# A 7x7 depthwise filter moved from VectorE to TensorE, with banded matrices streamed from HBM

## The chip, the cores and the metric

The kernel runs on one core of one Trainium2 chip. The metric is the device time of one execution in microseconds (us), the median of all its executions. Ratios are the mean time of one kernel's fast runs over that of the other's in the same rounds, so they are not quite the ratio of the medians that stand beside them.

## The reference

Eight images of 56 x 56 tokens with 192 channels, all in fp32, go through four layers. Each adds its result to its input, and each begins with a group norm. The change concerns layer 3:

```
y = conv_general_dilated(gn(x), dw_kernel, 'SAME', feature_group_count=192) + dw_bias   # 7x7, one filter per channel
y = (y - mean) * rsqrt(var + 1e-6) * ln_gamma + ln_beta                                 # over the channels
y = gelu(y @ w0 + b0) @ w1 + b1                                                         # 192 -> 768 -> 192
x = x + y * gamma                                                                       # gamma = 1e-6
```

One thing to keep in mind: with gamma at 1e-6 the comparison with the reference hardly sees layer 3.

## The kernel before

A program of the core goes image by image, layer by layer. The image lies in SBUF with channels on partitions, as two halves of 96. The filter is 49 multiply-adds per half on VectorE, over a padded copy of the image:

```
for k in range(2):
    pad = ...                        # GpSimd clears the border, ScalarE writes the normed image into it
    yk = y[:, k].rearrange("p (h w) -> p h w", w=W)
    for tap in range(49):
        i, j = divmod(tap, 7)
        win = pad[:, i:i + H, j:j + W]
        wt = vec("dw", 49 * k + tap, HC)
        if tap == 0:
            nc.vector.tensor_scalar(yk, win, wt, vec("dwb", k, HC), ALU.mult, ALU.add)
        else:
            nc.vector.scalar_tensor_tensor(yk, win, wt, yk, ALU.mult, ALU.add)
center_and_scale(y, ...)             # layer norm: TensorE, VectorE, ScalarE
for t in range(NTT): ...             # the MLP on TensorE, GELU on ScalarE, store of x
```

Of the kernel before, what the change touches and what calls it, by code (L numbers as in the profile page):

```python
# [18 lines left out]
NT = H * W          # tokens of one image  # L19
HC = 96             # channels are held as two halves of 96 partitions  # L20
TT = 392            # tokens per matmul: seven rows
NTT = NT // TT
D1 = 576            # expanded width of layer 0
DCH = [(0, 128), (128, 128), (256, 128), (384, 128), (512, 64)]
NSUB = D1 // 64
HEADS, HD, WN = 6, 32, 49
C2 = 384
EXP = 768

# Per-partition vectors, packed by the host as columns of one [128, NV] array.  # L30
# [5 lines left out]
    ("dw", 98), ("dwb", 2), ("g3", 2), ("be3", 2), ("b0", 6), ("b1", 2), ("ls", 2),  # L36
]
VOFF = {}
NV = 0
# [5 lines left out]
def _reversed(ap):  # L45
    """The access pattern that runs backwards over the last dimension."""
    dims = [list(d) for d in ap.ap]
    step, num = dims[-1]
    return bass.AP(ap.tensor, ap.offset + (num - 1) * step, dims[:-1] + [[-step, num]])
# [3 lines left out]
def kernel(ctx: ExitStack, tc: tile.TileContext, a: dict, out: bass.AP):  # L53
# [13 lines left out]
    # ---------------------------------------------------------------- constants  # L67
# [36 lines left out]
    # layer scale times its bias, so that (y + b1) * ls = y * ls + lsb  # L104
# [5 lines left out]
    # Toeplitz matrices of layer 0 and attention bias + mask of layer 1, made once and kept in HBM.  # L110
# [3 lines left out]
    # ---------------------------------------------------------------- helpers  # L114
    def gn_stats(x, pool, psum):
        """Per-channel scale and shift of the group norm over (H, W, 6 channels)."""
        st = pool.tile([HC, 2, NTT, 6], F32, name="gn_st")
        mv = pool.tile([HC, 2, 2], F32, name="gn_mv")
        for k in range(2):
            for t in range(NTT):  # L120
                nc.vector.bn_stats(st[:, k, t, :], x[:, k, bass.ts(t, TT)])
            nc.vector.bn_aggr(mv[:, k, :], st[:, k].rearrange("p t s -> p (t s)"))
        gm = psum.tile([HC, 2], F32, name="gn_ps", tag="gn_ps", bufs=1)
        nc.tensor.matmul(gm, gmat, mv[:, :, 0], start=True, stop=True)
        mean = pool.tile([HC, 2], F32, name="gn_mean")
        nc.vector.tensor_copy(mean, gm)
        d = pool.tile([HC, 2], F32, name="gn_d")
        nc.vector.tensor_tensor(d, mv[:, :, 0], mean, ALU.subtract)
        nc.vector.tensor_tensor(d, d, d, ALU.mult)
        nc.vector.tensor_tensor(d, d, mv[:, :, 1], ALU.add)  # L130
        gv = psum.tile([HC, 2], F32, name="gn_ps2", tag="gn_ps", bufs=1)
        nc.tensor.matmul(gv, gmat, d, start=True, stop=True)
        sc = pool.tile([HC, 2], F32, name="gn_sc")
        nc.scalar.activation(sc, gv, AF.Sqrt, bias=eps5[0:HC])
        nc.vector.reciprocal(sc, sc)
        sh = pool.tile([HC, 2], F32, name="gn_sh")
        nc.vector.scalar_tensor_tensor(sh, mean, -1.0, sc, ALU.mult, ALU.mult)
        return sc, sh

    def center_and_scale(X, P, NC, mean_w, eps, pool, psum):  # L140
        """X <- (X - mean) / sqrt(var + eps) over the channels (partitions x NC), in place."""
        vps = psum.tile([128, 2, 512], F32, name="ln_var", tag="ln_var", bufs=1)
        for t in range(NTT):
            g, j = divmod(t, 2)
            xs = X[:, :, bass.ts(t, TT)]
            mp = psum.tile([P, TT], F32, name="ln_mean", tag="ln_b", bufs=2)
            for k in range(NC):
                nc.tensor.matmul(mp, mean_w, X[:, k, bass.ts(t, TT)], start=(k == 0), stop=(k == NC - 1))  # L148
            nc.vector.tensor_tensor(xs, xs, mp.unsqueeze(1).to_broadcast([P, NC, TT]), ALU.subtract)  # L149
            sq = pool.tile([P, NC, TT], F32, name="ln_sq", bufs=2)  # L150
            nc.scalar.activation(sq, xs, AF.Square)  # L151
            for k in range(NC):
                nc.tensor.matmul(
                    vps[32 * g:32 * g + 32, j, 0:TT], mean_w[:, 0:32], sq[:, k, :],
                    start=(k == 0), stop=(k == NC - 1),
                )
        rs = pool.tile([128, 2, TT], F32, name="ln_rs", bufs=1)
        nc.scalar.activation(rs, vps[:, :, 0:TT], AF.Sqrt, bias=eps)
        nc.vector.reciprocal(rs, rs)
        for t in range(NTT):  # L160
            g, j = divmod(t, 2)
            xs = X[:, :, bass.ts(t, TT)]
            bp = psum.tile([P, TT], F32, name="ln_rstd", tag="ln_b", bufs=2)
            nc.tensor.matmul(
                bp, ones[32 * g:32 * g + 1, 0:P], rs[32 * g:32 * g + 1, j, :], start=True, stop=True
            )
            nc.vector.tensor_tensor(xs, xs, bp.unsqueeze(1).to_broadcast([P, NC, TT]), ALU.mult)

    # ---------------------------------------------------------------- set-up of layer 0
    def build_toeplitz():  # L170
        coef = dram.tile([2, D1, 112], F32, name="coef")
        with tc.tile_pool(name="tz", bufs=2) as pool, tc.tile_pool(name="tz_ps", bufs=2, space=PSUM) as psum:
# [6 lines left out]
            # powers of the decay, 0..55, then laid out by lag: column k is lag 55 - k  # L179
# [17 lines left out]
            for i in range(2):  # L197
# [19 lines left out]
                # Hankel rows by overlapping reads, turned into Toeplitz rows by a backward copy  # L217
# [9 lines left out]
    # ---------------------------------------------------------------- set-up of layer 1  # L227
    def build_bias_mask():
        with tc.tile_pool(name="bm", bufs=2) as pool, tc.tile_pool(name="bm_ps", bufs=1, space=PSUM) as psum:
            rev = pool.tile([WN, WN], F32, name="rev", bufs=1)  # L230
            nc.gpsimd.dma_start(rev, a["rev49"])
            # rows by reversed query: offsets (i', j') + (im, jm) into the reversed table
# [27 lines left out]
    # ---------------------------------------------------------------- layer 0  # L260
    def layer0(x, b):
        with ExitStack() as st:
# [16 lines left out]
            for c, (d0, M) in enumerate(DCH):  # L279
                # q * v by channel, in rows of 64 columns (the last 8 are zero)  # L280
# [9 lines left out]
                # o[w, d, h] = sum_w0 T1[w0, w] qv[w0, h] + sum_h0 qv[h0, w] T2[h0, h], as one  # L290
                # product per channel: rows 0..55 hold the w0, rows 64..119 the h0
# [43 lines left out]
                # gate, and the part of the output projection of these channels  # L335
# [16 lines left out]
    # ---------------------------------------------------------------- layer 1  # L352
    def layer1(x, b):
        with ExitStack() as st:
# [8 lines left out]
            # scores: heads of one 32-row group of the array share a bank, windows of a pair are  # L363
            # 64 partitions apart; the rows between them are zero
# [5 lines left out]
            def rolled(g):  # L370
                """(rows of the group, rows and columns of the image) of a rolled row of windows."""
# [5 lines left out]
            for g in range(8):  # L377
                bm = pool.tile([128, 3, 8 * WN], F32, name="bm")
                nc.sync.dma_start(bm.rearrange("p a b -> p (a b)"), bmask[g])
                # window after window, each of 7 x 7 tokens  # L380
# [61 lines left out]
                # keys onto partitions: et[m, (h % 3, pair, h // 3), query of both windows]  # L442
# [37 lines left out]
    # ---------------------------------------------------------------- layer 2  # L480
    def layer2(x, b):
        with ExitStack() as st:
# [11 lines left out]
            for m in range(3):  # L494
# [25 lines left out]
                # four running averages (their gain is applied to the sum)  # L520
# [32 lines left out]
    # ---------------------------------------------------------------- layer 3  # L553
    def layer3(x, b):
        with ExitStack() as st:
# [3 lines left out]
            y = pool.tile([HC, 2, NT], F32, name="y3", bufs=1)  # L559
            for k in range(2):  # L560
                pad = pool.tile([HC, H + 6, W + 6], F32, name="pad3")
                nc.gpsimd.memset(pad[:, 0:3, :], 0.0)
                nc.gpsimd.memset(pad[:, H + 3:H + 6, :], 0.0)
                nc.gpsimd.memset(pad[:, 3:H + 3, 0:3], 0.0)
                nc.gpsimd.memset(pad[:, 3:H + 3, W + 3:W + 6], 0.0)
                nc.scalar.activation(
                    pad[:, 3:H + 3, 3:W + 3], x[:, k].rearrange("p (h w) -> p h w", w=W), AF.Identity,
                    bias=sh[:, k:k + 1], scale=sc[:, k:k + 1],
                )
                yk = y[:, k].rearrange("p (h w) -> p h w", w=W)  # L570
                for tap in range(49):
                    i, j = divmod(tap, 7)
                    win = pad[:, i:i + H, j:j + W]
                    wt = vec("dw", 49 * k + tap, HC)
                    if tap == 0:
                        nc.vector.tensor_scalar(yk, win, wt, vec("dwb", k, HC), ALU.mult, ALU.add)
                    else:
                        nc.vector.scalar_tensor_tensor(yk, win, wt, yk, ALU.mult, ALU.add)  # L578
# [41 lines left out]
def _lay_out(inp):  # L620
    f = {k: np.asarray(v) for k, v in inp.items()}

    def cols(v, p, n):
        """A vector as n columns of p partitions, in 128 rows."""
# [19 lines left out]
        "dwb": cols(l3("dw_bias"), HC, 2), "g3": cols(l3("ln_gamma"), HC, 2), "be3": cols(l3("ln_beta"), HC, 2),  # L644
        "b0": cols(l3("b0"), 128, 6), "b1": cols(l3("b1"), HC, 2), "ls": cols(l3("gamma"), HC, 2),
    }
    for i in (1, 2):
# [3 lines left out]
    dw = np.zeros((128, 98), np.float32)  # L651
    dw[:HC] = l3("dw_kernel").reshape(49, 2, HC).transpose(2, 1, 0).reshape(HC, 98)
    v["dw"] = dw
# [17 lines left out]
        "w0": halves(l3("w0")), "w1": blocks(l3("w1")),  # L671
# [19 lines left out]
```

## Time and profile before

| | before |
|---|---|
| time, us (2 runs) | 14,654.9 and 14,661.6 |
| PE busy | 8,491.7 us, 58% |
| VectorE busy | 7,833.3 us, 53% |
| bytes read from HBM | 201 MB |
| filter stage, one image | 344.6 us, VectorE alone |

The prediction shows the page's lines and the filter stage. For contrast here are the windows of the first image on both sides of it: the end of layer 2, then the layer norm and the MLP of layer 3. The columns are: window, its length, busy time (and instructions) of PE, PEld, DVE, ACT, POOL, then granted TensorE clock, DMA share, GB/s.

```profile
1529.30:1559.30 30.00, 29.97 (x85) 14.45 (x84) 10.00 (x15) 2.19 (x4) 0.00 (x0) 0.93 0.00 0
...
1903.90:1955.60 51.70, 44.87 (x85) 13.81 (x85) 19.57 (x16) 16.29 (x22) 0.00 (x0) 0.67 0.00 0
1955.60:2083.30 127.70, 126.31 (x377) 67.18 (x376) 9.99 (x17) 41.67 (x69) 0.00 (x0) 0.98 0.06 17
```

TensorE sets the pace on both sides and VectorE in between. The stages do not overlap, so a time won or lost in the filter stage counts in full, eight times.

### The profile page before, as it was taken

How to read it: one execution, taken by the hardware profiler on the slowest of the kernel's cores; microseconds unless marked ns; L12 is line 12 of the kernel's file. 1: busy time of each engine (PE TensorE's matmuls, PEld its weight loads, DVE VectorE, ACT ScalarE, POOL GpSimd, SP SyncE). 2: the span in 40 equal slices, each digit the busy share in tenths (PEclk: the TensorE clock that was granted, in tenths of full speed). 3: DMA queues.
4: the chain of work that ended last, by engine and by line, in shares of the span. 5: the costliest groups of instructions: out<-in, count | busy, mean ns of one | idle time of the engine just before them, and what ended most of it. 6: DMA issues, size and time to landing. Idle time of an engine off the chain costs nothing.

```text
span 14692.5 us, 108024 instructions
## 1 busy us (share of the span) xinstructions
PE 8491.7 (58%) x46978; PEld 4935.2 (34%) x46978; DVE 7833.3 (53%) x6307; ACT 2537.9 (17%) x3928; POOL 170.7 (1%) x331
## 2 busy tenths in 40 slices
PE   2873278731887308873088631886338852388524
PEld 1642046410454105541055310553115431154312
DVE  2237832478324792247922488225872358623685
ACT  0211022210221102211022110221112111122111
POOL 2000000000000000000000000000000000000000
PEclk9776577765877658776577765867667676677756
DMA  7100011000110001100010000100001000010000
GB/s 134 29 12 9 0 26 24 14 7 0 26 24 14 7 0 26 24 14 7 0 35 15 14 7 1 34 18 11 7 3 33 18 11 7 5 40 10 9 0 7
DMA packets 107622, 249.45 MB, mean 17 GB/s; under 512 B 73238, under 2 KB 85812, under 8 KB 95724
## 3 DMA queue, kind: packets, MB, share of 16 engines
q1 hardware_dynamic: 103148, 234.09, 7.0%
q0 software_dynamic: 4000, 8.46, 0.2%
q8 instruction: 368, 6.03, 0.2%
q14 instruction: 106, 0.87, 0.0%
HBM read 201.38 MB, written 41.12 MB: 17 GB/s over the span
## 4 chain that ended last, share of the span: by engine, by line
PE 54%; DVE 38%; issue 3%; ACT 2%; DMA 0%; DVEq 0%; ACTq 0%; POOL 0%; SPq 0%; POOLq 0%
DVE y L578 17%; PE pj L273 10%; PE op L329 7%; PE y L345 5%; DVE mixed L519 5%; PE ph L588 4%; PE po L596 3%; PE tph L316 3%; PE mm L404 3%; PE mmv L416 2%; PE ln_mean L148 2%; PE et_ps L447 2%; PE ot L341 2%; DVE tmp L534 2%; PE po L546 2%
## 5 line engine op out<-in xcount | busy, mean ns | idle before, releaser
L578 DVE SCALAR_TENSOR_TENSOR y<-pad,vecs_sb,y 96x3136 f32<-96x3136 f32 x768 | 2610.0, 3475 | 0.6
L148 PE MATMUL ln_mean<-y,mean 96*96 96x392 f32 x256 | 128.7, 649 | 2648.4 <-DVE y L578 2648.4
L273 PE MATMUL pj<-xn,w_pqv_sb 96*128 96x392 f32 (+1 forms) x3840 | 1508.2, 544 | 35.5 <-DVE xn L268 33.9
L329 PE MATMUL op<-rt,lt 120*56 120x56 f32 x9216 | 1003.3, 303 | 223.3 <-DVE o L332 113.5
L329 PEld LDWEIGHTS op<-rt,lt 120*56 120x56 f32 x9216 | 904.0, 210 | 320.8 <-DVE o L332 141.4
L148 PEld LDWEIGHTS ln_mean<-y,mean 96*96 96x96 f32 x256 | 46.0, 203 | 2725.9 <-DVE y L578 2659.0
L273 PEld LDWEIGHTS pj<-xn,w_pqv_sb 96*128 96x128 f32 (+1 forms) x3840 | 705.5, 193 | 607.1 <-issue 164.9
L345 PE MATMUL y<-pp,w_o_sb 128*96 128x392 f32 (+1 forms) x1280 | 697.6, 682 | 231.0 <-DVE pp L342 231.0
L148 PE MATMUL ln_mean<-mixed,mean 128*128 128x392 f32 x384 | 189.0, 636 | 1071.9 <-DVE mixed L536 1070.6
L519 DVE SCALAR_TENSOR_TENSOR mixed<-pad,vecs_sb,mixed 128x3136 f32<-128x3136 f32 x192 | 670.1, 3490 | 5.7
L447 PE MATMUL et_ps<-ident,e 128*49 128x128 f32 x1536 | 349.1, 407 | 557.0 <-DVE e L441 556.1
L503 PE MATMUL pin<-xn,w_in_sb 96*128 96x392 f32 x768 | 339.2, 610 | 508.5 <-ACT pad L507 475.2
L342 DVE TENSOR_TENSOR pp<-pp,ot 128x392 f32<-128x392 f32 (+1 forms) x320 | 179.5, 561 | 829.1 <-PE ot L341 541.5
L332 DVE COPY o<-op 56x448 f32<-56x448 f32 x288 | 177.6, 617 | 829.2 <-PE op L329 829.2
L602 DVE TENSOR_TENSOR x<-x,z 96x392 f32<-96x392 f32 x128 | 72.0, 563 | 940.8 <-ACT z L600 940.8
L588 PE MATMUL ph<-y,w_sb 96*128 96x392 f32 x1536 | 568.0, 525 | 0.0
L350 DVE TENSOR_TENSOR x<-x,y 96x392 f32<-96x392 f32 x512 | 286.0, 559 | 466.6 <-PE y L345 454.8
L151 ACT ACTIVATE ln_sq<-y 96x784 f32<-96x784 f32 x64 | 54.8, 857 | 2768.8 <-DVE y L149 2739.5
L289 DVE TENSOR_TENSOR qv<-qs,vs 128x392 f32<-128x392 f32 (+1 forms) x320 | 180.2, 563 | 633.1 <-ACT vs L287 633.1
L596 PE MATMUL po<-hid,w_sb 128*96 128x392 f32 x1536 | 516.2, 492 | 0.0
L316 PE MATMUL tph<-ident,qv 64*56 64x64 f32 x4032 | 473.5, 296 | 40.2 <-ACT rt L312 34.7
L148 PEld LDWEIGHTS ln_mean<-mixed,mean 128*128 128x128 f32 x384 | 82.9, 234 | 1171.1 <-DVE mixed L536 1090.0
(157 smaller groups left out, 12471.6 us busy)
## 6 DMA issues: line engine op xcount, KB each, us to landing
lt<-toep SPq DMA_DIRECT2D x72, 896.0 KB, 6.9
rt<-toep SPq DMA_DIRECT2D x72, 784.0 KB
bm<-bmask SPq DMA_DIRECT2D x64, 588.0 KB, 3.7
x<-in_x_dram SPq DMA_DIRECT2D x16, 1176.0 KB, 8.2
out_dram<-x SPq DMA_DIRECT2D x64, 294.0 KB, 2.6
toep<-tzt SPq DMA_DIRECT2D x18, 896.0 KB, 6.2
hk<-coef SPq DMA_DIRECT2D x18, 784.0 KB
bmask<-bmt POOLq DMA_DIRECT2D x8, 588.0 KB, 3.1
```

The source lines that it names most:

```text
L148: nc.tensor.matmul(mp, mean_w, X[:, k, bass.ts(t, TT)], start=(k == 0), stop=(k == NC - 1))
L273: nc.tensor.matmul(ps[0:M], w_pqv[:, k, which, d0:d0 + M], xn[:, k, bass.ts(t, TT)], start=(k == 0), stop=(k == 1),)
L316: nc.tensor.transpose(tp[:, i, :], qv[q0:q0 + 64, :, 8 * grp + i], ident[q0:q0 + 64, q0:q0 + 64])
L329: nc.tensor.matmul(op[:, i, :], lt[0:120, d, :], rt[0:120, d, :], start=True, stop=True)
L345: nc.tensor.matmul(y, w_o[0:M, c, k * HC:(k + 1) * HC], pp[0:M], start=True, stop=True)
L404: nc.tensor.matmul(ps, w_qkv[:, k, c0:c0 + HC], xf[:, k, :], start=(k == 0), stop=(k == 1))
L447: nc.tensor.transpose(tp[:, j, :], e[:, 4 * i + j, :], ident)
L503: nc.tensor.matmul(ps.rearrange("p h w -> p (h w)"), w_in[:, k, m * 128:(m + 1) * 128], xn[:, k, bass.ts(t, TT)], start=(k == 0), stop=(k ...
L519: nc.vector.scalar_tensor_tensor(loc3, win, wt, loc3, ALU.mult, ALU.add)
L578: nc.vector.scalar_tensor_tensor(yk, win, wt, yk, ALU.mult, ALU.add)
L588: nc.tensor.matmul(ps, w0[:, k, m * 128:(m + 1) * 128], y[:, k, bass.ts(t, TT)], start=(k == 0), stop=(k == 1),)
L596: nc.tensor.matmul(ps, w1[:, m, k * HC:(k + 1) * HC], hid[:, m, :], start=(m == 0), stop=(m == 5))
```

## The change

The intent is to take the filter from VectorE to TensorE, which is busy for 3.86 of the 344.6 us of that stage. Two image rows (112 tokens) go onto partitions by transposes. For each channel a banded matrix turns those 112 inputs into two output rows; four matrices (j) cover the seven filter rows. A channel has only 28 pairs of rows, so its matmul fills 32 columns of the array, and four channels go to four column groups. The bands are made on the host and streamed from HBM; all 192 channels' bands are 39 MB. A 113th row of the contraction, all ones in z, carries the bias.

```diff
-            y = pool.tile([HC, 2, NT], F32, name="y3", bufs=1)
-            for k in range(2):  # ... pad, and 49 multiply-adds on VectorE
+            xp = ...   # normed image, one empty row above and below
+            z = pool.tile([128, C * ZS + 8], F32, name="z", bufs=1)       # 112 tokens x (channel, pair of rows)
+            # ... 58 transposes, 12 copies into z, borders cleared, ones in row 112
+            for T in range(C // 16):
+                k, p0 = divmod(16 * T, HC)
+                cv = psum.tile([128, 4, ZR], F32, name="cv", tag="ln_b")
+                for g in range(4):
+                    bd = pool.tile([ZR + 1, 4, 4 * ZR], F32, name="band", bufs=3)   # ZR = 112
+                    nc.sync.dma_start(bd, a["band"][4 * T + g])
+                    for j in range(4):
+                        for u in range(4):
+                            c = 16 * T + 4 * u + g
+                            nc.tensor.matmul(
+                                cv[32 * u:32 * u + 32, g, :], z[0:ZR + 1, c * ZS + j:c * ZS + j + 32],
+                                bd[:, u, j * ZR:(j + 1) * ZR], start=(j == 0), stop=(j == 3),
+                            )
+                yc = ...   # copy of cv, VectorE and ScalarE in turn
+                for u in range(4):
+                    nc.sync.dma_start(yd[...], yc[32 * u:32 * u + 28])    # to HBM, and back by channel:
+                if p0 == HC - 16:
+                    nc.sync.dma_start(y[:, k], yd[...])
```

The rest of the diff takes comments out, drops the filter weights from the resident constants and builds the bands on the host.

## The prediction

> **What bounds the kernel now.** I read the page's busy shares, then the chain of work that ended last, then that chain in order of time for one image, then windows of that image, and last the DMA queues and issues, because the change moves work from VectorE to a stream from HBM.
>
> ```profile
> PE 8491.7 (58%) x46978; PEld 4935.2 (34%) x46978; DVE 7833.3 (53%) x6307; ACT 2537.9 (17%) x3928; POOL 170.7 (1%) x331
> ...
> PE 54%; DVE 38%; issue 3%; ACT 2%; DMA 0%; DVEq 0%; ACTq 0%; POOL 0%; SPq 0%; POOLq 0%
> ...
> L578 DVE SCALAR_TENSOR_TENSOR y<-pad,vecs_sb,y 96x3136 f32<-96x3136 f32 x768 | 2610.0, 3475 | 0.6
> ```
>
> No engine is full over the whole span: the images run one after another, each through four layers, and within a layer one engine sets the pace. The filter of layer 3 is 768 VectorE instructions of 3.475 us, with VectorE idle only 0.6 us before all of them. The chain in time shows one image:
>
> ```profile
> 1529.34 29.94 PE po L546 x84
> 1559.85 4.30 DVE gn_st L121 x9
> ...
> 1581.16 20.43 DVE y L578 x7
> ...
> 1604.85 295.53 DVE y L578 x87
> 1900.40 3.49 DVE y L578
> 1903.94 5.61 PE ln_mean L148 x8
> ```
>
> Layer 2 ends at 1559.3 (1529.34 + 29.94); the layer norm behind the filter starts at 1903.9. Windows on those borders:
>
> ```profile
> 1559.30:1903.90 344.60, 3.86 (x8) 1.75 (x8) 339.55 (x123) 6.26 (x3) 1.63 (x8) 0.51 0.00 0
> ```
>
> The columns are busy PE, PEld, DVE, ACT, POOL, then granted clock, DMA share, GB/s. So the stage is 344.6 us per image, 8 x 344.6 = 2,757 us in all, VectorE alone; TensorE and the DMA engines do nothing in it. That is all that the change can win. A replacement must finish in under 344.6 us per image.
>
> [...] The change brings 384 loads of a band tile of 113 partitions (112 rows and one row for the bias). [...]
>
> [...]
>
> ```profile
> q1 hardware_dynamic: 103148, 234.09, 7.0%
> ...
> lt<-toep SPq DMA_DIRECT2D x72, 896.0 KB, 6.9
> rt<-toep SPq DMA_DIRECT2D x72, 784.0 KB
> ```
>
> Data packets, one per contiguous row: lt 72 x 64, rt 72 x 56, toep 18 x 64, hk 18 x 56 x 64, bm 64 x 128, out 64 x 192, x 16 x 96, coef 8 x 128 + 2 x 64, six constants 416 rows: 97,888. What is left of 103,148 is 5,260 completion packets. The 250 loads and stores whose partition count 16 divides account for 4,000; the other 90 (rt and hk, 56 partitions) for 1,260, which is 14 each. 14 is the largest divisor of 56 up to 16. [...]
>
> [...] The trace's packet records give the duration of one packet where it is not slowed by others: 66 ns for 1,568 bytes, 181 for 4,704, 467 for 12,544, 533 for 14,336. That is a line, 8.5 ns plus 27.3 bytes per ns[...]; within one engine the packets follow each other without a gap (in the stores to out the next starts 3 ns before to 2 ns after the last ends). With 16 engines at once the whole is less than 16 times that:
>
> ```profile
> 1368.00:1370.00 2.00, 0.00 (x0) 0.00 (x0) 1.97 (x2) 0.00 (x0) 0.00 (x0) 0.50 1.04 245
> 2684.00:2686.00 2.00, 0.00 (x0) 0.00 (x0) 2.00 (x5) 0.00 (x0) 0.00 (x0) 0.50 0.93 310
> ```
>
> [...]
>
> **The change part by part, for one image.**
>
> Removed: 96 multiply-adds of 3.475 us (333.6), two first taps of 1.905, two pad activations of 3.05 and their waits. All of the 344.6 us goes, except the group-norm statistics (11 us) that begin the stage in both.
>
> Added on VectorE, ScalarE and TensorE: two scalings (1.9 us each, as the xn rows take), 58 transposes of 96 x 112 and 12 copies of some 0.6 us, 768 matmuls of 112 columns, 12 copies of 128 x 448. The po chain runs 24 matmuls of 392 columns in 7.90 us at a clock of 0.98, 0.84 ns a column; 112 columns are then 0.09 us, or 0.19 at half clock (estimates). The 16 matmuls that one band feeds take 1.5 to 3 us even if the column groups overlapped not at all. All of this is small.
>
> Added on the queue: 48 band loads of 113 rows x 7,168 bytes (810 KB). One row is 8.5 + 7168 / 27.3 = 271 ns on one engine; 113 rows are 30.6 us. With three buffers there are always two loads queued behind the one that runs: the built program issues band n+3 when the 16 matmuls of band n are done, and each block's four stores to yd come behind the bands two ahead. So the one engine does not run dry, and the stream takes 48 x 30.6 = 1,469 us. The engine's share of the yd stores (two of 28 rows, 4 packets of 25 ns each, 48 times: 9.6 us) and of the first y load (6 x 467 ns: 2.8 us) is in the same ring: 12 us.
>
> Head: the first band waits for layer 2's last output matmul, because its buffer lies where layer 2's tiles were. So the stream starts at 1559.3 + 1.0 (x needs 1.0 us from issue to its first packet). Statistics and transposes lie beside it, for the first matmuls can wait until about +35 us while only three bands fill.
>
> Tail: after the last band 3 us of matmuls, 0.6 copy, four store issues at 0.45, 2.2 landing, and the second y load 6.6: about 15 us.
>
> Sum: 1 + 1,469 + 12 + 15 = 1,497 us in place of 344.6: +1,152 us per image. Everything before 1559.3 and after 1903.9 is unchanged, and the images do not overlap here. 14,658 + 8 x 1,152 = 23,876, rounded to 23,880 us.
>
> **The rivals.**
>
> 1. *All 16 engines carry the bands*[...]. For it: the author surely meant it so, and 245 GB/s would bring a band in 3.3 us. Then the stage would be some 34 us until the transposes are done, 45 further bands at 3.3 to 3.7 us, up to 12 block ends at 5 us where stores hold the queue, and the tail: 215 to 275 us instead of 344.6, a gain of 0.55 to 1.0 ms, ending at 13.65 to 14.1 ms. Against it: the 14 completions of a 56-row load.
>
> 2. *One engine, at another speed.* My packet times come from moments with other engines at work, but the fast ones are on a straight line of bytes, so I take them as the engine's own rate. [...] A lone engine [...] say 22 GB/s, gives 36.8 us and 26.3 ms. The 20.8 GB/s (310 / (16 x 0.93)) of the second window above is with 16 engines and some slow packets, so this is the less likely side.
>
> 3. *The queue adds bubbles*: the stores to yd wait for a copy, and bands behind them are not issued meanwhile. If the engine ran dry at each of 12 blocks for 8 us, 8 x 96 us = 0.8 ms more: 24.6 ms. Against it: two bands of 30 us each are queued at that moment.
>
> 4. *TensorE becomes the bound* by matmuls [...]. Even at 300 ns each, without overlap, 768 take 230 us, hidden under the stream [...]; under rival 1 it would cancel most of the gain.
>
> **Range and chances.** The answer is almost binary. I give the one-engine branch 0.92. Inside it the rate moves the time by 0.36 ms for 1 us of a band; 28 to 32.5 us and small bubbles give 22.9 to 24.9 ms, my range, for 8 times in 10. Rival 1 with a good outcome has 0.06, and 0.02 is left for it with its gain eaten by TensorE or the queue.
>
> **What would show it.** Right: in the filter's stage a DMA share near 0.06 (1 of 16) at 26 to 27 GB/s; a band landing every 30 to 31 us, and near 90 us from issue to landing with three queued; q1 with 113 + 1 packets per band load, so 384 single completions; the chain that ended last in layer 3 on DMA, with TensorE waiting for band; VectorE's busy time down by some 2.6 ms. Wrong: 113 + 16 packets per load, a share near 1, a band each 3 to 4 us. A band well off 30.6 us would mean that the engine's rate is mis-sized; a rate right but a stage longer than 48 bands would mean bubbles.

That the band loads of 113 rows run on one engine was an estimate of mine at that point: the trace of before shows 14 completions for each load of 56 rows, 14 being the largest divisor of 56 up to 16, and holds no load of 113 rows.

## The result, and the profile after

The changed kernel took 23,906.03 us (2 runs, 23,905.1 to 23,907.0) against 14,658.25; the ratio is 1.631, 95% interval 1.626 to 1.636.

From the page of the changed kernel: busy time by engine; the DMA queue of the sync engine; the chain that ended last, by engine and by line; and the group of the new matmuls (count, busy us, mean ns, then the idle time before them and what ended it).

```profile
PE 9217.6 (39%) x59730; PEld 5506.4 (23%) x59730; DVE 5283.6 (22%) x5635; ACT 2543.1 (11%) x4008; POOL 208.3 (1%) x315
...
q1 hardware_dynamic: 197100, 583.63, 8.1%
...
PE 35%; DMA 18%; SPq 17%; another core or an unknown queue 13%; DVE 12%; issue 2%; ACT 1%; DVEq 0%; ACTq 0%; POOL 0%; POOLq 0%
DMA band<-in_band_dram 18%; SPq L614 14%; PE pj L274 6%; PE op L330 4%; PE y L346 3%; DVE mixed L520 3%; SPq L600 2%; PE ph L629 2%; PE po L637 2%; PE tph L317 2%; PE mm L405 2%; PE cv L604 2%; PE mmv L417 1%; PE ln_mean L149 1%
...
L604 PE MATMUL cv<-band,z 113*32 113x112 f32 x12288 | 667.0, 393 | 11034.3 <-DMA band<-in_band_dram 11034.3
```

VectorE lost 2,550 us of work, as intended, and TensorE gained 726. But TensorE stood still for 11,034 us before the new matmuls, all of it for bands. (The count 12,288 is twice the 6,144 matmuls of the source: in this trace each of these fp32 matmuls shows as two instructions, while the 464 transposes, 58 an image, show as one each.)

The chain of the first image in order of time (start, length, what) shows the pace:

```profile
1522.44 29.95 PE po L547 x84
1552.52 32.64 DMA band<-in_band_dram
...
1615.85 1.72 PE cv L604 x32
1617.57 28.89 another core or an unknown queue
1646.50 1.72 PE cv L604 x32
1648.22 28.88 another core or an unknown queue
1677.14 1.77 PE cv L604 x32
...
3045.17 6.82 DMA y<-yd
...
3052.03 5.61 PE ln_mean L149 x8
```

The matmuls of one band (32 instructions) take 1.72 us, then TensorE waits until 30.65 us after the last band came, and so on: 1646.50 - 1615.85 = 30.65, 1677.14 - 1646.50 = 30.64. The words "another core or an unknown queue" are the profile's for a landing that it can't assign; the waits in the group above name the band. Blocks of the chain that it books on the sync queue's issues (L614) have the same inside: four bands with a block's stores take 1800.50 - 1677.14 = 123.4 us, 30.8 each. The stage runs from 1552.4 to 3052.0, 1,499.6 us in place of 344.6. One period as a window:

```profile
1646.00:1677.20 31.20, 1.77 (x36) 1.38 (x40) 0.00 (x0) 0.00 (x0) 0.00 (x0) 0.50 0.06 26
```

A DMA share of 0.06 is one engine of 16, and that one moves 26 GB/s. The queue's packets say the same: 197,100 - 103,148 = 93,952 more than before. Stores to yd (384 x (112 + 14)) and loads of y (16 x (96 + 16)) are 50,176 of them; the other 43,776 are 384 x 114, that is 113 rows and one completion per band. In the packet records the completions are packets of 4 bytes, 11,276 in this trace and 5,260 in that of before. A row of 7,168 bytes takes 273 ns in the median and 272 at the least.

### The profile page after: what moved, and what is told of

Read it like the earlier page. It is cut to its first block, busy times and chain, and to the rows that moved or that the text cites. A ratio compares the mean times of both kernels' runs of the same rounds, so it can differ in the third digit from the quotient of the medians.

```text
span 23905.2 us, 134629 instructions
## 1 busy us (share of the span) xinstructions
PE 9217.6 (39%) x59730; PEld 5506.4 (23%) x59730; DVE 5283.6 (22%) x5635; ACT 2543.1 (11%) x4008; POOL 208.3 (1%) x315
## 3 DMA queue, kind: packets, MB, share of 16 engines
q1 hardware_dynamic: 197100, 583.63, 8.1%
## 4 chain that ended last, share of the span: by engine, by line
PE 35%; DMA 18%; SPq 17%; another core or an unknown queue 13%; DVE 12%; issue 2%; ACT 1%; DVEq 0%; ACTq 0%; POOL 0%; POOLq 0%
DMA band<-in_band_dram 18%; SPq L614 14%; PE pj L274 6%; PE op L330 4%; PE y L346 3%; DVE mixed L520 3%; SPq L600 2%; PE ph L629 2%; PE po L637 2%; PE tph L317 2%; PE mm L405 2%; PE cv L604 2%; PE mmv L417 1%; PE ln_mean L149 1%
## 5 line engine op out<-in xcount | busy, mean ns | idle before, releaser
L604 PE MATMUL cv<-band,z 113*32 113x112 f32 x12288 | 667.0, 393 | 11034.3 <-DMA band<-in_band_dram 11034.3
L604 PEld LDWEIGHTS cv<-band,z 113*32 113x32 f32 x12288 | 509.3, 167 | 11195.2 <-DMA band<-in_band_dram 8747.5
L317 PEld LDWEIGHTS tph<-ident,qv 64*56 64x56 f32 x4032 | 397.9, 161 | 85.6 <-ACT rt L313 40.1
L448 PEld LDWEIGHTS et_ps<-ident,e 128*49 128x49 f32 x1536 | 262.2, 188 | 610.2 <-DVE e L442 563.9
L342 PEld LDWEIGHTS ot<-ident,o 56*128 56x128 f32 (+1 forms) x2240 | 282.8, 190 | 465.5 <-issue 350.3
L342 PE MATMUL ot<-ident,o 56*128 56x56 f32 (+1 forms) x2240 | 367.5, 295 | 24.6 <-ACT o L335 24.6
L405 PE MATMUL mm<-xr,w_qkv_sb 96*96 96x392 f32 x1024 | 371.2, 518 | 14.7 <-DVE xn L168 9.2
```

The lines of the kernel that those rows point to most:

```text
L317: nc.tensor.transpose(tp[:, i, :], qv[q0:q0 + 64, :, 8 * grp + i], ident[q0:q0 + 64, q0:q0 + 64])
L342: nc.tensor.transpose(ot[0:M, i, :], o[:, 0:M, 7 * t + i], ident[0:W, 0:W])
L405: nc.tensor.matmul(ps, w_qkv[:, k, c0:c0 + HC], xf[:, k, :], start=(k == 0), stop=(k == 1))
L448: nc.tensor.transpose(tp[:, j, :], e[:, 4 * i + j, :], ident)
L604: nc.tensor.matmul(cv[32 * u:32 * u + 32, g, :], z[0:ZR + 1, c * ZS + j:c * ZS + j + 32], bd[:, u, j * ZR:(j + 1) * ZR], start=(j == 0), s ...
```

## The experiments

The theory: 113 has no divisor from 2 to 16, so a band load runs on one DMA engine, and that alone makes the stage long. The rivals: the 311 MB of bands are too much whatever the engines; TensorE, granted a clock of 0.50 in the stage, comes right behind; the waits of the queue.

**112 rows and the bias row apart.** The same bytes, tile and matmuls, two transfers a band.

```diff
-                    nc.sync.dma_start(bd, a["band"][4 * T + g])
+                    nc.sync.dma_start(bd[0:ZR], a["band"][4 * T + g, 0:ZR])
+                    nc.sync.dma_start(bd[ZR:ZR + 1], a["band"][4 * T + g, ZR:ZR + 1])
```

> The same bytes, the same 113-row tile and the same matmuls, but each band comes by two transfers, 112 rows and then the one bias row. Theory (one engine of 16 because 113 has no divisor up to 16): the 112 rows run on 16 engines, a band lands every 3.3 to 3.8 us instead of 30.6, the filter stage takes 215 to 275 us, the time is 13.6 to 14.1 ms, under the kernel before. Rival a (the 311 MB of the stream, or HBM, are the bound): the time stays at 23.9 ms. Rival b (TensorE [...] is the bound just behind the stream): the stage stays above 345 us and the time above 14.66 ms.

Measured: 13,827.65 us, ratio to the kernel before 0.9435 (0.942 to 0.9451). The stage is 241.4 us. From its page, the sync queue, and a window in the middle of the stage:

```profile
q1 hardware_dynamic: 203244, 583.66, 17.2%
```

```profile
1620.00:1640.00 20.00, 9.04 (x176) 7.10 (x172) 0.62 (x1) 0.00 (x0) 0.00 (x0) 0.50 0.83 221
```

The queue has 203,244 - 197,100 = 6,144 packets more, 16 a band: 112 + 16 and 1 + 1 in place of 113 + 1. So the band's rows now run on 16 engines, and 221 GB/s are moved in place of 26. That rules the bytes out as the cause: the same 311 MB now fit into a stage that is shorter than the one on VectorE.

**118 rows.** The band gets five zero rows; 118 is 2 x 59.

```diff
-                    bd = pool.tile([ZR + 1, 4, 4 * ZR], F32, name="band", bufs=3)
+                    bd = pool.tile([118, 4, 4 * ZR], F32, name="band", bufs=3)       # matmuls read bd[0:ZR + 1]
```

> The band is padded with five zero rows to 118 = 2 x 59 rows, in one transfer; the matmuls read the first 113. 4% more bytes. Theory (largest divisor up to 16): two engines, 59 rows of 271 ns each, 16.0 us a band, 48 of them 768 us, the stage near 795 us in place of 1,500, the time 18.1 to 18.5 ms, and 118 + 2 packets a band. Rival a (bytes): 4% longer than the changed kernel's stage, 24.4 ms. Rival c (any other count than 113 is spread over all 16 engines): 14 ms as with 112 + 1 rows.

Measured: 18,321.17 us (one run). Chain, first image:

```profile
1528.91 29.94 PE po L547 x84
...
2348.81 7.16 DMA y<-yd
...
2356.01 5.61 PE ln_mean L149 x8
```

The stage is 2356.0 - 1558.9 = 797 us, forecast 795. The queue has 199,404 packets, 6 a band more than with 113 rows: 118 + 2 in place of 113 + 1. More bytes, two engines, half the time: with 113, 118 and 112 rows the count of completions is the largest divisor up to 16 (1, 2 and 16), and the stage takes 1,499.6, 797 and 241.4 us.

**One band for all.** No stream; the result is wrong.

```diff
+            bd = pool.tile([ZR + 1, 4, 4 * ZR], F32, name="band", bufs=1)    # loaded once per image, used by all matmuls
             for T in range(C // 16):
                 for g in range(4):
-                    bd = pool.tile(...); nc.sync.dma_start(bd, a["band"][4 * T + g])
```

> Wrong result on purpose: one band is loaded per image and all 768 matmuls of the filter use it, so the stream is gone and all else stays (transposes, matmuls, copies, stores, reload). It measures the stage without its stream. Theory: statistics and transposes 34 us, 48 times 1.72 us of matmuls as the changed kernel's trace shows them = 83 us, tail 15 us, together 120 to 140 us, the time 12.9 to 13.1 ms. If the stores' waits or the copies set the pace of a block, the stage is above 180 us and the time above 13.3 ms.

Measured: 12,615 us (one run), less than forecast. The stage without its stream is 1648.6 - 1559.8 = 88.9 us. The miss is the clock: I had taken 1.72 us a band from the changed kernel, whose granted clock is 0.50 in the window above, but in the run without the stream TensorE is granted 1.00 (the first window of the next experiment), and a band takes 0.82 us. So TensorE was not near being the bound of the changed kernel.

**The same, group after group.** What do the four column groups bring? Only the order of the matmuls changes.

```diff
-                    for j in range(4):
-                        for u in range(4):
+                    for u in range(4):
+                        for j in range(4):
```

> As the run with one band (wrong result on purpose, no stream), but the 16 matmuls of a band are issued group after group, so that four in a row go to the same column group. With the groups in turn, 128 instructions [...] took 3.27 us at full clock, 25.5 ns each. If column groups run beside each other, [...] the 1,536 instructions of an image 30 to 33 us more, the time 12.85 to 12.9 ms. If the 25.5 ns are only an issue pace and nothing overlaps, 12.6 ms as before. Rival: the order hardly matters, because the fourth is followed by another group.

Measured: 12,853.57 us (one run). A window of the matmuls in the run with groups in turn, then in this one:

```profile
1595.00:1615.00 20.00, 16.45 (x642) 15.16 (x640) 1.88 (x3) 1.06 (x2) 0.00 (x0) 1.00 0.25 55
```

```profile
1600.00:1620.00 20.00, 20.00 (x392) 20.00 (x389) 0.63 (x1) 1.06 (x2) 0.00 (x0) 1.00 0.16 34
```

Both at full clock. In turn: 16.45 us for 642 instructions, 25.6 ns each. Group after group: 20 us for 392, 51 ns each. So the order is worth a factor of 2.0, and the stage grows from 88.9 to 118.2 us. The time is the forecast one, but by luck: the forecast assumed a pace, which no trace had shown, for an instruction that follows another on its group. The start times in the two traces say 96 ns.

In turn, starts come in fours: three steps of 6 to 8 ns, then a longer one, and from a start to the fourth after it is 96 ns in the median. In the po chain, 24 fp32 instructions of 392 columns in 7.90 us, one starts every 329 ns, which is 94 ns for 112 columns (an estimate from this chain). So four instructions run beside each other, each at its own pace of 96 ns, and the four column groups bring 96 / 25.6 = 3.7. Group after group, the eight instructions of a group start within 413 ns in place of 8 x 96 = 766, so even there about two neighbouring groups overlap. (The trace does not name the groups; that the four are four groups is read from the order in the source.)

The 25.6 ns are a mean, of starts 6 to 8 ns apart and one long step. None of this shows in the changed kernel, where TensorE waits 28.7 us for a band in the mean (11,034.3 us for 384).

**Stores on ScalarE's queue.** Added to the 112 + 1 rows.

```diff
-                    nc.sync.dma_start(yd[...], yc[...])
+                    nc.scalar.dma_start(yd[...], yc[...])
```

> As the 112 + 1 rows, and the stores of the filter's result are issued from the ScalarE queue, so that no band load stands behind a store in the order of one queue. Theory (with 16 engines the three buffers hold only 11 us of stream, so a store that waits for a copy lets it run dry 12 times an image): 3 to 6 us a block, 36 to 72 us an image, 0.3 to 0.6 ms less than with 112 + 1 rows alone. If the stream is never dry, the same time within 0.5%.

Measured: 13,544.47 us, ratio 0.9242 (0.9228 to 0.9255), so 1.9% of the time before, or 35 us an image, less than 112 + 1 rows, just under the 36 to 72 us of the forecast; the stage is 204.9 us in place of 241.4. The chain of the 112 + 1 rows shows what went: copy, four store issues, only then the next band issues, then a wait for a band.

```profile
1593.41 0.64 DVE yc L611
1594.06 0.33 SPq L615
1594.43 0.39 SPq L615
1594.87 0.41 SPq L615
1595.32 0.42 SPq L615
1595.85 0.34 SPq L600
...
1597.75 12.46 DMA band<-in_band_dram
```

With 16 engines the queue's order matters. With one it did not: two bands of 30 us each were always waiting, and a band took 30.8 us with a block's stores and 30.65 without.

**Six buffers.** The filter's tiles go into a pool of their own, which is closed before the MLP's tiles are made, so that six bands fit.

```diff
-                    bd = pool.tile([ZR + 1, 4, 4 * ZR], F32, name="band", bufs=3)
+                    bd = cp.tile([ZR + 1, 4, 4 * ZR], F32, name="band", bufs=6)
```

> As the 112 + 1 rows with stores on ScalarE's queue, with six band buffers in place of three (the filter's tiles lie in a pool of their own, which the MLP's tiles take over). In that run the stream stood still while the first three bands waited for the transposes (DMA share 0.43 in the first 20 us). Theory: six bands fill the wait, 18 to 25 us an image less, 13.35 to 13.4 ms. If the stream's pace is all, no change from 13.54 ms.

Measured: 13,460.58 us, ratio 0.9181 (0.9169 to 0.9194): 0.6% of the time before, 11 us an image, and I had forecast 18 to 25. The stage is 196.9 us. Part of the head is won (the DMA share in the first 20 us is 0.71 in place of 0.43). From 1600 us to the tail the share is 0.90 to 1.00, so there the stream's own rate is the bound.

**112 rows, bias by VectorE.** The bias row is gone; VectorE adds the bias while it empties PSUM.

```diff
-                    nc.sync.dma_start(bd[ZR:ZR + 1], a["band"][4 * T + g, ZR:ZR + 1])
-                if T % 2 == 0:  nc.vector.tensor_copy(yc, cv)
-                else:           nc.scalar.copy(yc, cv)
+                nc.vector.tensor_tensor(yc, cv, dwb[:, 4 * T:4 * T + 4].unsqueeze(2).to_broadcast([128, 4, ZR]), ALU.add)
```

> As the six buffers, the bias row gone from the band: 112 rows in one transfer, the bias added by VectorE as it empties PSUM. Each engine has 7 rows a band[...]. If the stream goes at the pace of its busiest engine: 1/8 off 48 x 3.4 us, about 20 us an image, 0.16 ms less than six buffers. If the total rate bounds it (bytes 1% fewer): the same as six buffers within 0.3%.

Measured: 13,384.27 us, ratio 0.9131 (0.9118 to 0.9143): 0.5% less, about half of what the busiest engine would give and more than the total rate would. (The forecast's 1/8 is 7 rows an engine against 8 on the one that also brings the bias row, an estimate from 113 rows on 16 engines.) It tells nothing apart, since a transfer a band also went and all copies moved to VectorE.

**128 rows in one transfer.** As six buffers, 15 zero rows more.

```diff
-                    nc.sync.dma_start(bd[0:ZR], ...)
-                    nc.sync.dma_start(bd[ZR:ZR + 1], ...)
+                    nc.sync.dma_start(bd, a["band"][4 * T + g])          # bd has 128 rows
```

> As the six buffers, the band padded with zero rows to 128 and brought in one transfer: 8 rows on every engine, 13% more bytes, no transfer of its own for the bias row. If the busiest engine sets the pace: the same time as six buffers within 0.5%. If the total rate bounds the stream: 48 x 3.4 x 0.13 = 21 us an image more, 0.17 ms more.

Measured: 13,140.7 us, ratio 0.8961 (0.8949 to 0.8973), 2.4% under six buffers. Both theories fell: with 13% more bytes it is neither the same nor slower. Windows in mid-stream, of the 112 rows with the bias by VectorE and then of the 128 rows:

```profile
1620.00:1640.00 20.00, 11.07 (x208) 8.73 (x212) 1.25 (x2) 0.00 (x0) 0.00 (x0) 0.50 1.05 277
```

```profile
1600.00:1620.00 20.00, 13.64 (x272) 10.71 (x276) 0.62 (x1) 0.53 (x1) 0.00 (x0) 0.59 1.03 418
```

All engines are busy in both, and yet 418 GB/s are moved in place of 277. The packet records show it row by row: a row takes 419 ns in the median with 112 rows and 272 with 128, which is what one engine needs alone (273). A new theory was due: with 128 rows the engines do not get into each other's way. Which rows an engine gets the packet records do not say, so two runs test the theory from outside.

**113 to 128 rows and nothing else.** The changed kernel with one number changed.

```diff
-                    bd = pool.tile([ZR + 1, 4, 4 * ZR], F32, name="band", bufs=3)
+                    bd = pool.tile([128, 4, 4 * ZR], F32, name="band", bufs=3)       # matmuls read bd[0:ZR + 1]
```

> The changed kernel with one number changed: the band padded with zero rows from 113 to 128, 13% more bytes; three buffers and all stores on the sync queue as in the changed kernel. It separates the row count from the other edits of the fastest run. Theory (16 engines, and as in the fastest run 272 ns a row with all of them at work): 8 rows, 2.2 us a band, 48 of them 104 us; with head 32, 12 block ends of 4 to 6 us where the stores hold the queue, and tail 15 us the stage is 200 to 220 us, the time 13.5 to 13.7 ms, against 13.83 ms for 112 + 1 rows. If the fastest run owed its gain to buffers and one transfer a band: no better than 13.83 ms.

Measured: 13,445.41 us, ratio 0.915 (0.9136 to 0.9164), a little better than forecast; the stage is 1753.6 - 1564.1 = 189.5 us. The ends of the first image's stage:

```profile
1534.15 29.96 PE po L547 x84
...
1753.60 5.61 PE ln_mean L149 x8
```

Fifteen rows of zeros turn a loss of 63% into a gain of 8.5%. Three buffers and the stores' order are still in it, and it beats the 112 + 1 rows (0.9435) by 3.0%.

**120 rows.** As 128 rows with six buffers, with 120.

```diff
-                    bd = cp.tile([128, 4, 4 * ZR], F32, name="band", bufs=6)
+                    bd = cp.tile([120, 4, 4 * ZR], F32, name="band", bufs=6)
```

> The fastest run with 120 rows in place of 128: 8 rows an engine as there, on 15 engines, 6% fewer bytes; one transfer a band, six buffers. Theory [...]: a row takes over 380 ns in the median, a band 3.2 to 3.6 us, the time 13.35 to 13.5 ms. Rival (what counts is the number of rows an engine has, or one transfer a band): 272 ns a row and 13.1 to 13.2 ms.

Measured: 13,654.62 us, ratio 0.9299 (0.9283 to 0.9314), 3.8% slower than 128 rows and beyond my forecast in the theory's direction. A window in mid-stream:

```profile
1640.00:1660.00 20.00, 9.08 (x172) 7.11 (x176) 0.62 (x1) 0.00 (x0) 0.00 (x0) 0.50 0.98 240
```

A row takes 474 ns in the median. Eight rows an engine and one transfer a band are the same as with 128 rows, so neither of those explains the 128. What is shown: 128 rows are moved almost without mutual delay (with six buffers, 9 rows in 10 take at most 273 ns) and 112 and 120 are not (419 and 474 ns in the median). The place of the delay is not shown: it may lie on the side that reads HBM or on the side that writes SBUF, and no run changed one side alone. Why 120 rows are slower than 112 (474 against 419 ns) stays open too.

All times together, stages from the first image:

| kernel | rows x engines | time, us | ratio to before | stage, us |
|---|---|---|---|---|
| before | - | 14,658 | 1 | 344.6 |
| changed | 113 x 1 | 23,906 | 1.631 | 1,499.6 |
| 118 rows | 118 x 2 | 18,321 | one look | 797 |
| 112 + 1 | 112 x 16 | 13,828 | 0.9435 | 241.4 |
| + stores on ScalarE's queue | 112 x 16 | 13,544 | 0.9242 | 204.9 |
| + six buffers | 112 x 16 | 13,461 | 0.9181 | 196.9 |
| + no bias row | 112 x 16 | 13,384 | 0.9131 | 186.3 |
| 128 rows, six buffers, stores on ScalarE's queue | 128 x 16 | 13,141 | 0.8961 | 153.5 |
| the same, 120 rows | 120 x 15 | 13,655 | 0.9299 | 221.1 |
| changed, 128 rows only | 128 x 16 | 13,445 | 0.915 | 189.5 |
| one band (wrong result) | none | 12,615 | one look | 88.9 |

The engines of every row are counted from completion packets, as above; 120 rows, for one, have 135 packets a band, 120 + 15. The kernel with 128 rows, six buffers and stores on ScalarE's queue beats both kernels.

## Why the prediction was right

The forecast was 23,880 us and the time is 23,906, 0.1% off. Step by step:

- *What can be won is 344.6 us an image.* It held: outside the stage nothing moved by more than a few us an image.
- *One engine for 113 rows.* It held, exactly, by the count of packets. It was my estimate from the 14 completions of a 56-row load in the trace of before. 113, 118 and 112 rows then showed 1, 2 and 16 completions, again the largest divisor up to 16.
- *The rate.* The line through the uncontended packets gave 271 ns for a row; measured 273. Had I divided a 16-engine rate by 16 (245 / 16 = 15.3 GB/s), I would have forecast 53 us a band; the uncontended packets were the right ones to take: the lone engine's rows of 7,168 bytes took 273 ns, 26.3 GB/s.
- *The sum.* Stream, stores in the same queue, head and tail: 1,497 us forecast, 1,499.6 measured. The terms hold one by one, to 4 us: the first band lands 33 us after the stage's begin, 2 more than its 31 of transfer (forecast 1); from there to the last landing are 47 periods of 30.95, so 1,485 for 48 (forecast 1,469 + 12); the tail is 12 (forecast 15). Periods of 30.65 us against 30.6; 30.8 with the stores. The share of 0.06 at 26 GB/s is there. The first three bands' matmuls came at 33, 63 and 94 us after the stage's begin, which is the "near 90 us" for the third of three queued loads, though the page gives no landing time for them.
- *The chain on DMA, TensorE waiting.* It held in substance. The profile spreads the wait over three names, "DMA band", "SPq" and an unknown queue, so the share by engine (DMA 18%) understates it; the idle time before the matmuls is the better witness.
- *Rival 1* gave 13.65 to 14.1 ms for 16 engines, and the 112 + 1 rows took 13.83. *Rival 3's* bubbles were absent with one engine but real with 16, where taking them out gave 35 us an image. *Rival 4's* figure was too high: at full clock the whole stage without the stream is 88.9 us.
- *Two slips that cost nothing here.* The "24 matmuls" in 7.90 us are 24 instructions, two to a matmul, so without overlap a band's 32 instructions would take 32 x 0.19 = 6 us at half clock (an estimate from those 7.90 us), and not up to 3. The measured 1.72 us come in only because the column groups overlap (3.7 times in the run with one band). And 1 us of a band is 384 bands, 0.38 ms, not 0.36.

What the prediction did not foresee: that "16 engines" is not one rate. Its 3.3 to 3.7 us a band were near for 112 rows (3.7 at the 221 GB/s of the first such run, 2.9 at the 277 of the last), and 128 rows take 2.2 us (917,504 bytes at 418 GB/s). The packets of the kernel before already held a hint. Its 128-row loads (bm, 4,704 bytes a row) take 181 ns in the median and 179 at the least, as if each engine were alone. Its 96-row loads (x, 12,544 bytes) take 848 against 467, and its 64- and 56-row transfers (lt, rt and toep, 14,336 bytes) 1,093 against 533. The prediction used the least of each and did not ask why only some loads reach it. It is a hint, not a proof, since the row sizes differ.

## What to carry to other kernels

Before a load is sized, ask how many DMA engines its partition count gets, and prove it from a profile by counting completion packets (here 1 with 113 rows, 2 with 118, 15 with 120, 16 with 112 and 128). A row more or less can cost a factor of 16 in engines (26 against 221 GB/s here); a few rows of padding, up to 128, can be the cheapest edit in the kernel. Price a stream from packets of the same state it will run in: lone packets for a lone engine (273 ns a row here), crowded ones for 16 (419 ns with 112 rows). And when an unseen factor is removed, look again at what it hid: here the order of stores and loads in one queue, which cost nothing before and 2% after.
